# Two image layers on one core: the filling of the first pipeline rearranged

## The chip, the core and the metric

The kernel runs on one core of a Trainium2 chip. The time is the device time of one execution in microseconds (us). Before the change it is 3877.8 us, the median of three runs (3875.0 to 3879.05). The core has a matrix engine (PE, with weight loads shown apart as PEld), a vector engine (DVE), a scalar engine for activations (ACT), a general engine (POOL) and a queue engine (SP) that issues most transfers. Transfers move on 16 DMA engines shared by all queues. SP's transfers are plain copies. POOL issues those that add what they bring to what lies at the destination (accumulating transfers).

## What is computed

Input `x` has two images of 768 channels on 64 x 64 points. Two layers follow each other, each with a residual:

```python
x = x + mamba(_gn(x))      # layer 0
x = x + attention(_gn(x))  # layer 1
```

`_gn` is a group norm over 32 groups of 24 channels, with statistics over an image. Layer 0, cut to what matters:

```python
x = hs @ in_proj_w.T                          # 768 -> 1536 channels
xs = depthwise_conv3x3(x) + conv_b            # 9 taps per channel
xs = xs * sigmoid(xs)
dt, Bs, Cs = split(xs @ x_proj_w.T)           # 48 + 4 + 4
delta = softplus(dt @ dt_w.T + dt_b)
states = scan(exp(delta * A), delta * u * Bs) # along the 4096 points, 4 states
y = sum(states * Cs) + D * u
y = layernorm(y) * ln_g + ln_b                # over 1536 channels
out = y @ out_proj_w.T                        # 1536 -> 768
```

Layer 1 multiplies the normalized image by `W_qkv`, weighs it with a softmax over 12 heads, and multiplies it by `W_out`. The change does not touch it.

## The kernel before

An image is cut into 8 tiles of 8 rows (512 points); the two images make 16 tiles. The 1536 channels are 12 chunks of 128. A quantity number `g` counts tile times 12 plus chunk, 192 in all. One call of `step(g)` (line 894) does one piece of every stage of the pipeline for different numbers: the input product and row carry for number `n = g + 17`, the convolution taps for `a = g + 15`, the scan for `g`, and the output product for `g - 12`. The order is written out by hand (`tc.manual_schedule()`); each engine works through its own instructions in that order and waits where one needs another's result. The text counts the first steps as step 0 (`g = -17`) to step 15 (`g = -2`). In these, the filling, there is no scan and no output product.

Ahead of the filling (lines 876 to 892): 48 pieces of image 1 are loaded (`gn_load`, line 141) and DVE takes their statistics (`gn_piece`, L153). `gn_finish` (line 223) aggregates them per chunk (L225) and returns five parts of `gn_parts` (line 157). These average over the groups by matrix products with two constant matrices (`gavg_in`, loaded on L168; `gsel_in`, L174). In the four parts each matrix is loaded twice, by SP, into buffers taken from a pool of 46 (`slots`, with `take` and `give`). ACT then normalizes the six chunks of tile 0 (`norm_x`, L297) and computes the exponentials of `A_log` (L891, L892).

A step of the filling does, in this order:

- SP loads the input weights of the next number (`load_wi`, L303) into one of four buffers.
- PE multiplies image row 0 (`row0`, L325) and then the tile (`in_proj`, L336). Row 0 itself is loaded and normalized on ACT in step 0 (L318, L320).
- SP loads three pieces of image 2 (L148). DVE takes their statistics one step later, behind the taps.
- The taps of number `a`: ACT writes the middle tap into a PSUM bank (`tap_act`, L374). PE adds one tap by a product with a diagonal matrix that ACT made (`diag`, L369; `taps_pe`, L401). DVE adds the other seven (`taps_dve`, L415), the last into a buffer `u`. There is one such bank, so the taps of the next number wait for these.
- ACT evicts the input product with its carried rows (`in_proj_evict`, L348 to L351).
- Every fourth step ACT applies SiLU to four numbers between two table loads (`silu`, L420), and PE multiplies them by the projection weights (`x_proj_pair`, L427).

From number 15 on (`AHEAD`) the taps are divided in another way: ACT multiplies two or three taps into buffers `tm` (`taps_act`, L386). POOL adds them to each other by accumulating transfers (`taps_dma_sum`, L392) and adds the sum to `u` (`taps_dma`, L395). `DMA_TAPS`, `PE_TAPS` and `FILL_TAPS` name the taps.

The output weights are prepared in the filling too. Four loads (L242) bring all of them. In step 7 PE multiplies them by `ln_g` and `ln_b` (L250), 24 products of two rows by 384 columns. ACT copies the two rows (L254); PE then makes the output bias (L258) and the mean row spread over all partitions (L262). POOL scales each of the 12 chunks and subtracts the mean (L266, L267). SP stores them, two a step (L270), to a buffer in memory from which `load_wo` reads later.

When the filling ends, its buffers (`wg` among them) are given up and those of the scan take their place (`bc`, `ysum`, `tm`, `da`, `s`, lines 1056 to 1064). In the step of `g = -1` SP loads the rows of B and C spread over all partitions (`load_bc`, L447). In the step of `g = 0` DVE computes the first state product (L489), the first scan (L491), and so on.

Of the kernel before, what the change touches and what calls it, by code (L numbers as in the profile page):

```python
# [14 lines left out]
P = 128  # L15
# [4 lines left out]
NS = 4  # L20
# [28 lines left out]
PE_TAPS = ((), (1,), (), (1,))  # L49
FILL_TAPS = (1,)  # L50

# [15 lines left out]
def both_layers(  # L67
# [15 lines left out]
    nc.sync.dma_start(xsum, xsum_in)  # L83
    pick = wp.tile([2, P + 1], F32, name="pick")
    nc.sync.dma_start(pick, pick_in)
    xp_w = r0.tile([P, KI, XD2], F32, name="xp_w")
# [51 lines left out]

    pieces = {}

    def gn_load(b, v):
        k, h = divmod(v, L // 512)
        if b == 0:
            pieces[b, v] = take()
        else:
            tag, bufs = (("delta", 3), ("sq", 3), ("du", 2))[v % 8 // 3]
            pieces[b, v] = wk.tile([P, 512], F32, tag=tag, name=f"xg{b}_{v}", bufs=bufs)
        nc.sync.dma_start(pieces[b, v], xv[b][:, k, h * 512 : (h + 1) * 512])  # L148

    def gn_piece(b, v):  # L150
        k, h = divmod(v, L // 512)
        piece = pieces.pop((b, v))
        nc.vector.bn_stats(st_in[b][:, k, h, :], piece)  # L153
        if b == 0:
            give(piece)

    def gn_parts(name, mv, mean, rstd, then):


        st = {"held": []}  # L160

        def load(what):
            if what in st:
                return
            if what == "avg":
                st["held"] = [take()]
                st["avg"] = st["held"][0][:, : KM * G].rearrange("p (k g) -> p k g", g=G)
                nc.sync.dma_start(st["avg"], gavg_in)  # L168
            else:
                st["held"] = [take(), take()]  # L170
                st["sel"] = []
                for h, t in enumerate(st["held"]):
                    t = t[:G, : KM // 2 * P].rearrange("g (k p) -> g k p", p=P)
                    nc.sync.dma_start(t, gsel_in[:, h * (KM // 2) : (h + 1) * (KM // 2), :])  # L174
                    st["sel"] += [t[:, k, :] for k in range(KM // 2)]

        def done(what):
            st.pop(what)
            for t in st["held"]:
                give(t)  # L180

# [28 lines left out]
        def end():  # L210
            nc.vector.reciprocal(rstd, d)
            then()

        nothing = lambda: None
# [7 lines left out]

    def gn_finish(b):
        for k in range(KM):
            nc.vector.bn_aggr(mv_in[b][:, k, :], st_in[b][:, k, :, :])  # L225
        mean = gp.tile([P, KM], F32, name=f"xmean{b}")

        def then():
            nc.vector.tensor_mul(xbias[b], mean, xscale[b])
            nc.vector.tensor_scalar_mul(xbias[b], xbias[b], -1.0)  # L230
            nc.vector.tensor_scalar_mul(stats1[b][:, :, 2 * NT], mv_in[b][:, :, 0], -1.0)

        return gn_parts(f"x{b}", mv_in[b], mean, xscale[b], then)

    HM = DM // 2

    def out_weights_load(sp):
        wg = sp.tile([P, KI, DM], F32, name="wg")  # L240
        for k in range(0, KI, 3):
            nc.sync.dma_start(wg[:, k : k + 3, :], out_wT[k * P : (k + 3) * P, :].rearrange("(k p) m -> p k m", p=P))  # L242
        return wg

    def out_weights(sp, wg):

        gb = psO.tile([P, 2, 512], F32, tag="po", name="pgb")
        for e in range(2):
            for k in range(KI):
                nc.tensor.matmul(  # L250
                    gb[:2, e, :HM], pc[:, k, PC_G : PC_B + 1], wg[:, k, e * HM : (e + 1) * HM], start=(k == 0), stop=(k == KI - 1)
                )
        rows = sp.tile([2, 2, HM], F32, name="gb_rows")
        nc.scalar.copy(rows, gb[:2, :, :HM])  # L254
        rv = rows.rearrange("r e m -> r (e m)")
        pb = psS.tile([P, 512], F32, tag="st", name="pbo")
        for m in range(KM):
            nc.tensor.matmul(pb[:, m : m + 1], rv[:, m * P : (m + 1) * P], pick[:, P : P + 1], start=True, stop=True)  # L258
        nc.scalar.copy(bias_o, pb[:, :KM])
        wm = psO.tile([P, 2, 512], F32, tag="po", name="pwm")  # L260
        for e in range(2):
            nc.tensor.matmul(wm[:, e, :HM], pick[:, :P], rows[:, e, :], start=True, stop=True)  # L262
        wmean = sp.tile([P, 2, HM], F32, name="wmean")
        nc.scalar.copy(wmean, wm[:, :, :HM])
        for k in range(KI):
            nc.gpsimd.tensor_scalar_mul(wg[:, k, :], wg[:, k, :], pc[:, k, PC_G : PC_G + 1])  # L266
            nc.gpsimd.tensor_sub(wg[:, k, :], wg[:, k, :], wmean.rearrange("p e m -> p (e m)"))  # L267

# [42 lines left out]


    def row0(n):

        if n == 0:
            x0s["tile"] = take()
            x0s[0] = x0s["tile"][:, : KM * W].rearrange("p (k w) -> p k w", w=W)
            nc.sync.dma_start(x0s[0], xv[0][:, :, :W])  # L318
            for k in range(KM):
                nc.scalar.activation(  # L320
                    x0s[0][:, k, :], x0s[0][:, k, :], AF.Identity, bias=xbias[0][:, k : k + 1], scale=xscale[0][:, k : k + 1]
                )
        p0 = psZ.tile([P, 512], F32, tag="pz", name=f"pa0_{n}")
        for k in range(KM):
            nc.tensor.matmul(p0[:, :W], wis[n][:, k, :], x0s[0][:, k, :], start=(k == 0), stop=(k == KM - 1))  # L325
        nc.scalar.copy(carry[n][:, 1, :], p0[:, :W])
        if n == KI - 1:
            give(x0s.pop("tile"))
# [30 lines left out]
    def dma_taps(a):  # L359
        return DMA_TAPS[a % 4] if a >= AHEAD else ()  # L360

    def pe_taps(a):
        return PE_TAPS[a % 4] if a >= AHEAD else FILL_TAPS

# [16 lines left out]
    def taps_act(a):  # L381
        xs, c = xs_bufs[a % 2], a % KI
        tms[a] = (tm_bufs[a % 2], tm_bufs[2], tm_bufs[3 + a % 2])
        for tm, j in zip(tms[a], dma_taps(a)):
# [6 lines left out]
    def taps_dma_sum(a, q):  # L391
        nc.gpsimd.dma_start(tms[a][0], tms[a][q], accum_op=ALU.add)  # L392

    def taps_dma(a):
        nc.gpsimd.dma_start(us[a], tms.pop(a)[0], accum_op=ALU.add)  # L395

# [476 lines left out]
    norms = {}  # L873
    N_PIECE = KM * (L // 512)
    PER_STEP = 3
    with tc.manual_schedule():
        for v in range(N_PIECE):
            gn_load(0, v)
            gn_piece(0, v)
        for k in range(KM):  # L880
            load_x(0, k)
        load_wi(0)
        nc.sync.dma_start(xp_w, xp_wP)
        nc.sync.dma_start(dt_w, dt_wP)
        for load, pe, dve in gn_finish(0):
            load()
            pe()
            dve()
        for k in range(KM):
            norm_x(0, k)  # L890
        nc.scalar.activation(neg_a, pc[:, :, PC_A : PC_A + NS], AF.Exp)  # L891
        nc.scalar.mul(neg_a, neg_a, -1.0)  # L892

        def step(g, prep=None):
# [4 lines left out]
            if n + 1 < NQ0:  # L899
                load_wi(n + 1)  # L900
            elif NQ0 <= n + 1 < NQ0 + N_TAIL:
# [3 lines left out]
            if n < KI:  # L905
                row0(n)
            for q in range(v * PER_STEP, min((v + 1) * PER_STEP, N_PIECE)):
                gn_load(1, q)
# [19 lines left out]
            if BEHIND < g <= NQ0 + BEHIND and (g - BEHIND) % 4 == 0:  # L928
                out_evict(g)
            for q in range((v - 1) * PER_STEP, min(v * PER_STEP, N_PIECE)):  # L930
                if q >= 0:
                    gn_piece(1, q)
            if BEHIND + 2 < g and (g - BEHIND) % 4 == 2:
# [33 lines left out]
            elif n < NQ0 + N_TAIL:  # L967
# [4 lines left out]
                for k in {3: [0], 4: [1], 5: [2, 3, 4, 5]}.get(d[2], []):  # L972
                    norm_x1(0, d[1] + 1, k)
            if AHEAD <= a + 1 < NQ0:
                taps_act(a + 1)
# [9 lines left out]
            if do_b:  # L985
                du(g)
            late_tap = AHEAD <= a < NQ0 and len(dma_taps(a)) > 2
            if late_tap:
# [3 lines left out]
            if 0 <= g - 2 < NQ0:  # L992
                y_dma(g - 2, 1)
            if AHEAD <= a < NQ0 and not late_tap:
                taps_dma(a)
            if AHEAD <= a + 1 < NQ0:
                taps_dma_sum(a + 1, 1)
# [37 lines left out]
            if do_silu:  # L1035
                for q in range(0, 4, 2):
                    x_proj_pair(a - 4 + q)
            if (v - 1) * PER_STEP == N_PIECE:
                norms[g + 2] = gn_finish(1)
# [7 lines left out]
        with tc.tile_pool(name="l0st", bufs=1, side="right") as sp:  # L1047
            wg = out_weights_load(sp)
            for g in range(-AHEAD - 2, -1):
                step(g, (lambda: out_weights(sp, wg)) if g == -AHEAD + 5 else None)  # L1050
                if g >= -AHEAD + 7:
                    for k in ((g + AHEAD - 7) * 2, (g + AHEAD - 7) * 2 + 1):
                        if k < KI:
                            out_weights_store(wg, k)

# [173 lines left out]
```

## Time and profile before

| what | us |
|---|---|
| median of the three runs | 3877.8 |
| lowest and highest | 3875.0, 3879.05 |
| the profiled execution | 3880.97 |
| its span | 3879.2 |
| PE busy | 3643.6 |
| DVE busy | 2792.9 |
| ACT busy | 2459.8 |
| POOL busy | 1657.2 |
| first matrix product of row 0 starts | 63.87 |
| first state product starts | 227.60 |

All places in the profile are us from the start of the span. A row such as `L336 PE` belongs to line 336 of the kernel. The chain of waits is followed back from the last instruction, at each point to what released it; its pieces show start, length and what. A product in 32 bit is two records of PE. The granted clock is the share of PE's full clock in a stretch.

### The profile page before, as it was taken

To read this page: it belongs to the slowest core of one execution; us is meant where nothing else is said; L and a number is where in the kernel's file an instruction comes from. 1 tells how busy PE (TensorE), PEld (TensorE's weight loads), DVE (VectorE), ACT (ScalarE), POOL (GpSimd) and SP (SyncE) were. 2 spreads that over 40 slices of the span, in tenths; PEclk is the share of its full clock that TensorE was granted. 3 is DMA by queue.
4 is the path that set the end of the run, shared out by engine and by line. 5 is a ranking of instruction groups with operands and counts; after the bars stand their busy time and mean duration, and the time that the engine had idled before them with its cause. 6 is when DMAs were issued, how large, how long until landed. Compare 5 with 4: busy or idle time off the path is not lost.

```text
span 3879.2 us, 32882 instructions
## 1 busy us (share of the span) xinstructions
PE 3643.6 (94%) x9798; PEld 1512.8 (39%) x9798; DVE 2792.9 (72%) x2339; ACT 2459.8 (63%) x4667; POOL 1657.2 (43%) x1494
## 2 busy tenths in 40 slices
PE   4977999999999999999999999999999999998999
PEld 2422333333333333333433333333344444444444
DVE  5699999999999999999999999987400520005311
ACT  1378888888898888888888888886423511123000
POOL 0435556555655655655555655554300011111222
PEclk9988999999999999999999999999999999999999
DMA  7466898888888889889888898886543245442454
GB/s 278 160 177 134 187 205 180 201 202 194 203 182 200 205 188 207 179 202 213 172 203 183 202 206 184 198 176 168 146 126 129 68 145 154 150 140 83 142 179 154
DMA packets 321574, 679.65 MB, mean 175 GB/s; under 512 B 37378, under 2 KB 45572, under 8 KB 317300
## 3 DMA queue, kind: packets, MB, share of 16 engines
q0 software_dynamic: 139248, 253.56, 38.2%
q1 hardware_dynamic: 182148, 424.00, 33.4%
q8 instruction: 78, 1.28, 0.1%
q14 instruction: 100, 0.82, 0.1%
HBM read 393.77 MB, written 55.31 MB: 116 GB/s over the span
## 4 chain that ended last, share of the span: by engine, by line
DVE 45%; PE 34%; ACT 7%; issue 6%; DMA 5%; POOL 3%; SPq 0%; DVEq 0%; POOLq 0%; ACTq 0%
DVE s L491 17%; PE mm L665 13%; DVE acc L415 9%; PE mm L638 9%; DVE da L498 8%; DVE s L489 7%; PE pa L336 3%; PE po L551 3%; DMA tm<-tm 2%; PE pq L638 2%; DMA u<-tm 2%; POOL ysum L478 1%; DMA u<-ysum 1%; DVE u L563 1%; ACT da L466 1%
## 5 line engine op out<-in xcount | busy, mean ns | idle before, releaser
L551 PE MATMUL po<-u,w 128*128 128x512 f32 x2304 | 1047.8, 605 | 69.1 <-DVE u L563 68.7
L336 PE MATMUL pa<-u,w 128*128 128x512 f32 (+1 forms) x2304 | 1040.0, 601 | 0.0
L491 DVE TENSOR_TENSOR_SCAN s<-da,s 128x2052 f32<-128x2052 f32 x192 | 851.1, 4433 | 19.2 <-DVE s L489 0.5
L551 PEld LDWEIGHTS po<-u,w 128*128 128x128 f32 x2304 | 431.5, 192 | 673.8 <-issue 569.1
L336 PEld LDWEIGHTS pa<-u,w 128*128 128x128 f32 x2304 | 430.4, 192 | 591.4 <-issue 529.0
L478 POOL TENSOR_TENSOR ysum<-da 128x1024 f32<-128x1024 f32 x192 | 396.7, 2066 | 533.1 <-DVE da L498 506.9
L415 DVE SCALAR_TENSOR_TENSOR acc<-xs,pc,acc 128x512 f32<-128x512 f32 x753 | 567.8, 754 | 70.3 <-PE acc L401 50.3
L466 ACT ACTIVATE da<-dl,neg_a 128x512 f32<-128x512 f32 x768 | 489.6, 713 | 0.0
L660 POOL TENSOR_TENSOR w<-w,at 128x768 f32<-128x768 f32 x96 | 141.0, 1470 | 814.9 <-DMA w<-woutP 562.5
L392 POOL DMA_DIRECT2D tm<-tm x310 | 273.9, 885 | 500.5 <-ACT tm L386 444.9
L489 DVE TENSOR_TENSOR s<-du,bc 128x2048 f32<-128x2048 f32 x192 | 438.8, 2285 | 66.0 <-POOL du L470 63.8
L498 DVE TENSOR_TENSOR da<-s,bc 128x2048 f32<-128x2048 f32 x192 | 440.0, 2292 | 6.3
L485 POOL DMA_DIRECT2D u<-ysum x384 | 391.7, 1314 | 0.5 <-POOL ysum L478 0.3
L665 PE MATMUL mm<-u,w 128*128 128x512 f32 x684 | 320.8, 596 | 0.0
L386 ACT ACTIVATE tm<-xs,pc 128x512 f32<-128x512 f32 x487 | 317.7, 718 | 2.8 <-DMA tm<-tm 2.8
L674 DVE TENSOR_TENSOR u<-mm,u 128x512 f32<-128x512 f32 x59 | 40.8, 692 | 337.8 <-PE mm L665 337.8
L374 ACT ACTIVATE acc<-xs,pc 128x512 f32<-128x512 f32 x192 | 132.6, 690 | 211.7 <-DVE u L415 210.8
L470 POOL TENSOR_TENSOR du<-dl,u 128x512 f32<-128x512 f32 x192 | 258.7, 1348 | 0.0
L395 POOL DMA_DIRECT2D u<-tm x177 | 218.7, 1235 | 83.5 <-DMA tm<-tm 64.5
L665 PE MATMUL mm<-v,w 128*128 128x512 f32 x468 | 225.7, 593 | 0.0
L638 PE MATMUL mm<-u,w 128*128 128x512 f32 x456 | 214.4, 594 | 0.0
L665 PEld LDWEIGHTS mm<-u,w 128*128 128x128 f32 x684 | 129.3, 191 | 167.6 <-issue 167.4
(206 smaller groups left out, 4060.1 us busy)
## 6 DMA issues: line engine op xcount, KB each, us to landing
u<-ysum POOLq DMA_DIRECT2D x384, 256.0 KB, 5.8
tm<-tm POOLq DMA_DIRECT2D x310, 256.0 KB, 4.7
w<-in_wP SPq DMA_DIRECT2D x192, 384.0 KB, 4.3
w<-wo_dr SPq DMA_DIRECT2D x192, 384.0 KB, 5.1
u<-x SPq DMA_DIRECT2D x254, 256.0 KB, 4.3
u<-tm POOLq DMA_DIRECT2D x177, 256.0 KB, 5.8
w<-qkvP SPq DMA_DIRECT2D x96, 384.0 KB, 3.1
w<-woutP SPq DMA_DIRECT2D x96, 384.0 KB, 3.7
```

What stands on the lines that cost most here:

```text
L336: nc.tensor.matmul(pa[:, :nn], w[:, k, :], xts[i, k][:, :nn], start=(k == 0), stop=(k == KM - 1))
L386: nc.scalar.activation(tm.rearrange("p (h w) -> p h w", w=W), xs[:, dy : dy + TR, dx : dx + W], AF.Copy, scale=pc[:, c, PC_W + j : PC_W + ...
L415: nc.vector.scalar_tensor_tensor(dst, xs[:, dy : dy + TR, dx : dx + W], pc[:, c, PC_W + j : PC_W + j + 1], acc, ALU.mult, ALU.add)
L466: nc.scalar.activation(das[g % 2][:, n, 1:], deltas[g], AF.Exp, scale=neg_a[:, c, n : n + 1])
L478: nc.gpsimd.tensor_add(ysum[:, 0 : 2 + g % 2 : 1 + g % 2, :], da[:, 0:2, 1:], da[:, 2:4, 1:])
L485: nc.gpsimd.dma_start(us[g], ysums(g, n), accum_op=ALU.add)
L489: nc.vector.tensor_mul(s[:, :, 1:], dus.pop(g).unsqueeze(1).to_broadcast([P, NS, TL]), bc[:, :NS, :])
L491: nc.vector.tensor_tensor_scan(sf, das[g % 2].rearrange("p n l -> p (n l)"), sf, 0.0, ALU.mult, ALU.add)
L498: nc.vector.tensor_mul(das[g % 2][:, :, 1:], s[:, :, 1:], bc[:, NS:, :])
L551: nc.tensor.matmul(po[:, e, :], w[:, kk, e * P : (e + 1) * P], us[i * KI + k], start=(k == 0), stop=(k == KI - 1))
L638: nc.tensor.matmul(pa, w[:, k, :], x1s[b, j, k], start=(k == 0), stop=(k == KM - 1))
L665: nc.tensor.matmul(po, w[:, k, :], w1s[b, k, j], start=(k == 0), stop=(k == KM - 1))
```

## The change

- **Constants.** `gn_parts` gets `keep`: for image 1 each of the two constant matrices is loaded once and kept until the end. They are loaded directly behind the 48 pieces, ahead of tile 0, the weights and the rest.
- **Order ahead of the filling.** The load of row 0 and of input weights 1 and 2 go ahead of the filling; row 0 is normalized on DVE (`norm_x0`). The exponentials of `A_log` come after step 0.
- **Statistics of image 2.** Half of the 48 pieces are loaded ahead of the filling into the pool's buffers, and their statistics taken ahead of the taps. The other 24 go one or two a step.
- **Taps of the filling.** PE's tap 1 goes; taps 0 and 2 go to ACT and accumulating transfers, in buffers from the pool. DVE has six taps instead of seven.
- **Input weights** are loaded up to two steps ahead in the filling.
- **Output weights.** The four loads go to steps 2 to 5. The two rows are computed in three column groups of 256 (partitions 0, 32 and 64 of the result), in step 7; bias and mean follow in step 8, with a `pick` of 128 rows. ACT scales the chunks, POOL subtracts. One or two chunks a step, from step 8 to 15; their stores come a step later.

```diff
-FILL_TAPS = (1,)
+FILL_TAPS = (0, 2)
...
     def gn_load(b, v):
         k, h = divmod(v, L // 512)
-        if b == 0:
+        if v < N_EARLY[b]:
             pieces[b, v] = take()
...
+    def out_weights_load(wg, k):
+        nc.sync.dma_start(wg[:, k : k + 3, :], out_wT[k * P : (k + 3) * P, :].rearrange("(k p) m -> p k m", p=P))
+    MG = 2 * P
+    def out_weights_rows(wg, rows):
         gb = psO.tile([P, 2, 512], F32, tag="po", name="pgb")
-        for e in range(2):
-            for k in range(KI):
+        for k in range(KI):
+            for j in range(KM // 2):
                 nc.tensor.matmul(
-                    gb[:2, e, :HM], pc[:, k, PC_G : PC_B + 1], wg[:, k, e * HM : (e + 1) * HM], start=(k == 0), stop=(k == KI - 1)
+                    gb[32 * j : 32 * j + 2, 0, :MG], pc[:, k, PC_G : PC_B + 1], wg[:, k, j * MG : (j + 1) * MG],
+                    start=(k == 0), stop=(k == KI - 1),
                 )
+        for j in range(KM // 2):
+            nc.scalar.copy(rows[32 * j : 32 * j + 2, :], gb[32 * j : 32 * j + 2, 0, :MG])
+    def out_weights_mean(rows, wmean, pick):
         pb = psS.tile([P, 512], F32, tag="st", name="pbo")
+        wm = psO.tile([P, 2, 512], F32, tag="po", name="pwm")
+        for j in range(KM // 2):
+            for e in range(2):
+                m = 2 * j + e
+                nc.tensor.matmul(pb[:, m : m + 1], rows[:, e * P : (e + 1) * P], pick[:, j, P : P + 1], start=True, stop=True)
+            nc.tensor.matmul(wm[:, j // 2, j % 2 * MG : (j % 2 + 1) * MG], pick[:, j, :P], rows, start=True, stop=True)
+        nc.scalar.copy(wmean[:, : 2 * MG], wm[:, 0, :])
+        nc.scalar.copy(wmean[:, 2 * MG :], wm[:, 1, :MG])
         nc.scalar.copy(bias_o, pb[:, :KM])
...
-        for k in range(KI):
-            nc.gpsimd.tensor_scalar_mul(wg[:, k, :], wg[:, k, :], pc[:, k, PC_G : PC_G + 1])
-            nc.gpsimd.tensor_sub(wg[:, k, :], wg[:, k, :], wmean.rearrange("p e m -> p (e m)"))
+    def out_weights_scale(wg, wmean, k):
+        nc.scalar.activation(wg[:, k, :], wg[:, k, :], AF.Copy, scale=pc[:, k, PC_G : PC_G + 1])
+        nc.gpsimd.tensor_sub(wg[:, k, :], wg[:, k, :], wmean)
...
+    def norm_x0():
+        for k in range(KM):
+            nc.vector.tensor_scalar(
+                x0s[0][:, k, :], x0s[0][:, k, :], xscale[0][:, k : k + 1], xbias[0][:, k : k + 1], ALU.mult, ALU.add
+            )
...
     def dma_taps(a):
-        return DMA_TAPS[a % 4] if a >= AHEAD else ()
+        return DMA_TAPS[a % 4] if a >= AHEAD else FILL_TAPS
     def pe_taps(a):
-        return PE_TAPS[a % 4] if a >= AHEAD else FILL_TAPS
+        return PE_TAPS[a % 4] if a >= AHEAD else ()
...
-        tms[a] = (tm_bufs[a % 2], tm_bufs[2], tm_bufs[3 + a % 2])
+        tms[a] = (tm_bufs[a % 2], tm_bufs[2], tm_bufs[3 + a % 2]) if a >= AHEAD else (take(), take())
...
+    at = [0, 2, 3, 5, 6, 8, 9, 11, 12, 14, 15, 17, 18, 20, 21, 23, 24]
+    by_step = [range(N_PIECE // 2 + p, N_PIECE // 2 + q) for p, q in zip(at, at[1:])]
     with tc.manual_schedule():
         for v in range(N_PIECE):
             gn_load(0, v)
             gn_piece(0, v)
+        gn_aggregate(0)
+        parts = gn_finish(0)
+        for load, pe, dve in parts[:2]:
+            load()
         for k in range(KM):
             load_x(0, k)
         load_wi(0)
+        load_x0()
+        for n in (1, 2):
+            load_wi(n)
+        for v in range(N_EARLY[1]):
+            gn_load(1, v)
         nc.sync.dma_start(xp_w, xp_wP)
         nc.sync.dma_start(dt_w, dt_wP)
-        for load, pe, dve in gn_finish(0):
-            load()
+        for load, pe, dve in parts:
             pe()
             dve()
+        norm_x0()
         for k in range(KM):
             norm_x(0, k)
-        nc.scalar.activation(neg_a, pc[:, :, PC_A : PC_A + NS], AF.Exp)
-        nc.scalar.mul(neg_a, neg_a, -1.0)
+        for v in range(N_EARLY[1]):
+            gn_piece(1, v)
...
-            if AHEAD <= a < NQ0 and not late_tap:
+            if 0 <= a < NQ0 and not late_tap:
                 taps_dma(a)
-            if AHEAD <= a + 1 < NQ0:
+            if 0 <= a + 1 < NQ0:
                 taps_dma_sum(a + 1, 1)
...
+            first = -AHEAD - 2
+            ready_w = {8: (0,), 9: (1, 2), 10: (3,), 11: (4, 5), 12: (6, 7), 13: (8, 9), 14: (10,), 15: (11,)}
+            prep = {7: lambda: out_weights_rows(wg, rows), 8: lambda: out_weights_mean(rows, wmean, pick)}
+            for v in range(AHEAD + 1):
+                if 2 <= v < 6:
+                    out_weights_load(wg, 3 * (v - 2))
+                step(first + v, prep.get(v))
+                if v == 0:
+                    nc.scalar.activation(neg_a, pc[:, :, PC_A : PC_A + NS], AF.Exp)
+                    nc.scalar.mul(neg_a, neg_a, -1.0)
+                for k in ready_w.get(v, ()):
+                    out_weights_scale(wg, wmean, k)
+                for k in ready_w.get(v - 1, ()):
+                    out_weights_store(wg, k)
+            for k in ready_w[AHEAD]:
+                out_weights_store(wg, k)
```

## The prediction

> **What bounds the kernel now.** I read the page first (busy shares and forty slices), then busy time by stage, then the chain of waits in order of time through the first 260 us.
>
> ```profile
> PE 3643.6 (94%) x9798; PEld 1512.8 (39%) x9798; DVE 2792.9 (72%) x2339; ACT 2459.8 (63%) x4667; POOL 1657.2 (43%) x1494
> PE   4977999999999999999999999999999999998999
> ```
>
> PE carries the kernel; only the first slices leave it idle. The change touches only them. Busy time by stage:
>
> ```profile
> 39.70:63.90 24.20, 7.00 (x49) 6.72 (x49) 4.12 (x20) 6.73 (x12) 0.00 (x0) 1.00 1.02 365
> 128.10:158.30 30.20, 29.32 (x92) 11.80 (x91) 7.07 (x10) 3.81 (x9) 10.62 (x6) 0.89 0.24 75
> 227.60:380.00 152.40, 103.90 (x283) 39.89 (x282) 146.24 (x105) 125.95 (x228) 82.35 (x76) 0.81 0.66 133
> 380.00:2500.00 2120.00, 2038.85 (x5365) 810.45 (x5363) 2054.72 (x1354) 1823.36 (x3428) 1241.06 (x1151) 0.99 0.88 196
> ```
>
> (Columns: stretch, length, PE, PEld, DVE, ACT, POOL busy, clock, DMA share, GB/s.) From the first state product (DVE L489 at 227.6) on, DVE is 96 to 97% busy, so nothing there absorbs an earlier start: every us that 227.6 moves should reach the end. So I price that moment, called S. The chain to it:
>
> ```profile
> 40.39 7.33 DMA u<-gavg_in
> 57.33 4.33 ACT u L297 x6
> 61.66 1.28 ACT L891
> 63.39 0.43 ACT u L320
> 102.18 1.01 PE acc L401 x2
> 128.98 15.59 PE pgb L250 x48
> 144.59 0.80 ACT gb_rows L254
> 146.92 1.82 PE pwm L262 x4
> 148.74 2.75 PE pa L325 x12
> 151.50 6.81 PE pa L336 x12
> ```
>
> The group norm waits 7.3 us for its constants behind 2.7 MB of loads. ACT then serves six norms, a table load and image row 0 before PE starts at 63.87. Each step costs 7.5 us (row 0 1.28, product 5.21, tap 1.01). The output weights interrupt PE for 128.98 to 148.74. The page's rows of DMA queues and issues price the operation that the change adds to the filling (queue, packets, MB, share; then KB each and median us to landing):
>
> ```profile
> q0 software_dynamic: 139248, 253.56, 38.2%
> ...
> tm<-tm POOLq DMA_DIRECT2D x310, 256.0 KB, 4.7
> ...
> u<-tm POOLq DMA_DIRECT2D x177, 256.0 KB, 5.8
> ```
>
> **The change part by part.** I laid the changed order out engine by engine, each in its own order, with these durations.
>
> *Constants first.* SP issues them right behind image 1's pieces, so they land with the last piece, near 40. The averages then wait only for the six aggregates (end 41.2): 47.83 becomes 41.0, gain 6.8. The 9.5 us of averages to bias stay. The small load dropped at the start is worth 0 to 0.4; I take 0.
>
> *Row 0 on DVE, exponentials after step 0.* Six 128x64 operations on DVE cost about 1 us (the 128x6 ones cost 0.17 each), while ACT runs the six norms. Row 0 (2.8 at half pace, as now) starts near 51.3 and the first product after the sixth norm, 50.5 + 4.33 = 54.8, against 66.69. Cumulative gain 11.9. The table load and exponentials (1.8) move under step 1's product. Weights 1 and 2 and row 0 go ahead of 24 pieces; all land before use.
>
> *Half of image 2's statistics ahead.* 24 pieces x 256 KB at 404 GB/s (the rate of 20 to 40 us) are 15.6 us of queue, 24 x 0.635 = 15.2 us of DVE, from 51.3 to 66.5. Two more pieces queue behind them and two weight loads, so the first taps start near 68; step 2 needs them only then. Free, and each step keeps 1.5 pieces instead of 3 (0.9 us of DVE less).
>
> *Taps 0 and 2 by ACT and accumulating DMA, none on PE.* A step loses PE's 1.01, one of seven DVE taps (0.79) and ACT's diagonal (0.40). It gains two ACT products (1.94/3 = 0.65 each) and two POOL issues (L392 0.885, L395 1.235), with the accumulate's landing between them on POOL. PE then needs 1.28 + 5.21 = 6.5 a step, DVE 6 x 0.79 + 0.72 for ACT's product = 5.5, ACT 3.4. So PE bounds, and step 6's product, which ends at 117.2 now, ends at 100.2: cumulative gain 17.
>
> *The accumulate chain* is the new wait. POOL issues add a, then sum a+1, and add a+1 waits until sum a+1 has landed. The adds gate the SiLU of steps 6, 10 and 14, and behind SiLU stand ACT's product, its eviction and PE's x projection. An accumulate of 256 KB takes 38.2% x 3879 / 967 (253.56 MB in pieces of 256 KB) = 1.53 us of all DMA engines. Landing runs from 3.3 (best) over 4.7 (median) to 11.8 us. From the best landing 3.3 - 0.885 - 1.53 = 0.9 is latency, from the median 2.3; I take 1.4. One round is then issue 1.2 + 2 x 1.53 + 1.4 = 5.7 us alone, under 6.5. But in steps 2 to 5 SP now loads 1152 KB of output weights a step: with 384 KB of weights and 1.5 pieces that is about 5 us of DMA a step, plus 3.1 of accumulates, in 6.5 us. Sharing doubles the transfers: 1.2 + 6.1 + 1.4 = 8.7 a round. With the first sum issued at 70 and landed at 75, the fourth add is issued at 75 + 3 x 8.7 = 101 and lands at 107; ACT was ready for it at 99. PE's x projection waits from 100.2 to 107.7. So from step 6's product to step 7's: 7.5 + 1.87 + 1.28 + 5.2 + 2.9 for a slow clock after the wait = 18.8, against 10.9 now (117.2 to 128.1): loss 7.9, cumulative 9.1. Ends: a gain of 2.6 (5.7 a round, no wait) and a loss of 17 (11 a round). I take 7.9, as the load queue is full there. After step 6 POOL's subtractions stand between sums and adds; with 1.8 each they fit into the landing.
>
> The Trainium skill ("DMA: Bandwidth & Descriptors", section on queues, rings and completion order) says that each DMA engine round-robins between queues packet by packet. That speaks against this change, since loads would not yield to accumulates; no row of this trace has both queues isolated. By that rule the loss of 7.9 stands; if accumulates went first, the gain of 2.6 would.
>
> *Output weights' rows.* 72 records at 256 columns, 0.32 x 256/384 = 0.215 each, are 15.5 us one after another, or 5.2 with three column groups side by side. Row: L427, two groups of 64 columns, 8 records in 1.94 us instead of 8 x 0.43 = 3.4 (5.21 / 12 = 0.43 is a record of 512 columns). I take 5.2; the other end is 15.5. The means follow a step later (2.7 us on PE, counted there), so ACT's copies no longer stop PE, and the slow clock behind them (2.75 + 6.81 instead of 1.28 + 5.21) goes. From step 7's product to step 8's: 128.1 to 158.3 = 30.2 now, 5.2 + 1.28 + 5.2 = 11.7 after: gain 18.5 (8.2 by the other end), cumulative 27.6.
>
> *Scaling moved from POOL to ACT.* POOL loses 12 x 2.20. ACT gains 12 copies of 128x768 between 0.80 (L264) and 1.1 (0.78 for 512 columns, scaled up); I take 0.95. ACT's load over steps 8 to 15 becomes 8 x 3.4 + 2 x 5.1 (SiLU and tables) + 11.4 + 4.7 (norms) + 1.2 = 55 us, more than PE's 45. In order, with the waits on evictions, the means' 2.7 and one slow-clock stretch behind step 11's three norms (2.9), step 8's product to step 15's takes 59.6 (158.3 to 214.7 = 56.4 now): loss 3.2, ends a gain of 4 and a loss of 8.
>
> The same slow clock is in the Trainium skill ("TensorE: Matmul & The Clock Gate", Part 1): half rate after an idle window of about 3.4 us. Here row 0's 12 records took 2.82 us after idling and 1.45 in a run of work. By the rule an idle of 2 us would cost nothing and one of 7 about 2 to 3.
>
> *Stores a step late; the state products' inputs.* The last store (weights 11) now follows step 15's product on ACT, subtraction 1.8 and store 3.4 (page: 4.2 to landing). SP has the loads of B and C behind it, and their buffer lies where the weights lay. POOL's clearing of the decay buffers waits there too. From step 15's product, near 190: sum and copies to 193, the last copy at 195, subtraction 197, store 200, loads (median 6.5) 206. That is 15.6 against 214.7 to 227.6 = 12.9: loss 2.7, ends 0 and 8. SP's weight loads stand behind stores that wait for POOL; they are issued two steps ahead, which covers it.
>
> **Sum.** 17.0 - 7.9 + 18.5 - 3.2 - 2.7 = 21.7, so S at 206. The profiled execution is 3880.97 (span 3879.2), 3.2 above the median 3877.8. 3880.97 - 21.7 = 3859.3, so 3856 for a median.
>
> **The rivals.**
> 1. *The accumulates are never late* (5.7 to 6.5 a round). Speaks for it: median landing 4.7 with DMA 88% busy. Against: the load queue is full in steps 2 to 5. S near 198: 3880.97 - 29 - 3.2 = 3848.
> 2. *Half the gain:* groups run one after another (+10.3), or rounds of 9.5 to 10. S near 217: 3867. Against the first: L427.
> 3. *Slower: the accumulate chain sets the fill.* With rounds of P throughout, the last sum is issued at 70 + 14 P and S follows 16 us later (subtraction, store, loads): S = 86 + 14 P. It decides from P = 10.1; at 11 S is 240, 3890. For it: landings up to 11.8. Against: after step 6 loads fall to some 2.5 us a step.
> 4. *The gain is taken back* between 227.6 and 380 (clock 0.81, PE 68% busy), where PE's lead over DVE is rebuilt: no change, 3877. Against: DVE 96% busy there.
>
> **How the numbers follow.** Forecast (3851 to 3862) 0.48, rival 1 0.27, rival 2 0.13, rival 3 0.07, rival 4 0.05. Slower 0.07, same 0.05, faster 0.88; 0.2% (7.8 us) is about what a measurement can tell. Range 3842 to 3872: from S at 192 (no wait anywhere, ACT at 0.80 a copy) to S at 222 (groups one after another), which leaves some 0.17 out.
>
> **What would show it.** Averages at 41, first product near 55, steps of 6.5 up to step 6, a wait of ACT's L420 for the add's DMA at step 6, rows of some 5 us, S near 206, and 3650 us from S to the end as now. I am wrong if SiLU waits in every group, if the rows take 15 us, or if that last stretch grows.

## The result and the profile after

Median 3870.1 us (8 runs, 3864.9 to 3875.8) against 3879.4 (8 runs): ratio 0.9977, 95% interval 0.9967 to 0.9986, that is 5 to 13 us faster. The profiled execution has a span of 3866.9 us, 12.3 less than before. Forecast was a gain of 21.7 and a median near 3856: the direction holds, the size is too large, and 3870.1 lies above the 3851 to 3862 that were given the largest chance.

The page's busy shares and slices, then the queue and issue rows of the changed kernel:

```profile
PE 3631.4 (94%) x9794; PEld 1511.2 (39%) x9794; DVE 2783.4 (72%) x2331; ACT 2480.1 (64%) x4691; POOL 1655.0 (43%) x1512
...
PE   5867999999999999999999999999999999998999
...
q0 software_dynamic: 143568, 261.42, 40.2%
...
tm<-tm POOLq DMA_DIRECT2D x310, 256.0 KB, 4.7
u<-tm POOLq DMA_DIRECT2D x177, 256.0 KB, 5.9
```

PE gets to work within the first slice (5 instead of 4). Queue 0 carries 7.9 MB more: the 30 added accumulates of 256 KB. Busy time by stage (columns as in the prediction: stretch, length, PE, PEld, DVE, ACT, POOL, clock, DMA share, GB/s), from the averages to product 0, to product 6, 7, 8 and 15, to the first state product (S), to the second, and the run:

```profile
40.72:60.83 20.11, 17.16 (x74) 12.81 (x75) 12.74 (x37) 4.94 (x9) 0.00 (x0) 1.00 1.04 373
60.83:103.40 42.57, 40.86 (x147) 22.12 (x147) 33.94 (x50) 19.91 (x44) 6.21 (x7) 0.96 1.06 349
103.40:122.66 19.26, 13.18 (x35) 5.93 (x38) 8.80 (x13) 6.63 (x12) 4.32 (x5) 0.73 0.62 138
122.66:134.63 11.97, 11.97 (x99) 6.10 (x99) 6.11 (x9) 4.09 (x10) 1.72 (x2) 1.00 0.43 100
134.63:196.38 61.75, 53.49 (x156) 24.73 (x155) 36.89 (x52) 44.80 (x77) 32.03 (x25) 0.92 0.81 213
196.38:211.53 15.15, 13.09 (x33) 5.07 (x31) 5.18 (x8) 14.19 (x26) 5.87 (x7) 1.00 0.64 196
211.53:229.81 18.28, 6.91 (x18) 2.50 (x16) 14.07 (x15) 10.45 (x20) 5.92 (x6) 0.76 0.92 250
```

```profile
380.00:2500.00 2120.00, 2040.67 (x5373) 811.36 (x5372) 2053.49 (x1355) 1826.78 (x3433) 1240.27 (x1152) 0.99 0.89 196
```

Product 6 ends at 103.4 (before 117.2), product 7 at 122.7 (128.1), product 8 at 134.6 (158.3), product 15 at 196.4 (214.7), and S is at 211.5 (227.6): 16.1 gained at S where 21.7 was forecast. Then the first scan step takes 18.3 us instead of 14.8, so that the second state product has a gain of only 12.6. From there to the end both kernels take the same time within 0.3 us. The chain of waits (start, length, what) shows three places where accumulates or sums are waited for:

```profile
97.47 1.21 DMA u<-u
98.67 8.45 issue
107.14 3.62 DMA u<-u
110.78 0.73 ACT u L437
...
113.53 2.75 PE pa L337 x12
116.28 6.38 PE pa L348 x12
122.66 5.29 PE pgb L255 x72
...
177.97 6.75 DMA u<-u
...
213.50 4.65 issue
218.15 6.96 DMA tm<-tm
...
225.67 3.31 DMA u<-tm
```

The first (97 to 111) is the one of the prediction, before the SiLU of step 6. The row called "issue" is POOL standing before an add until the sum that it issued at 97.47 has landed, 9.1 us later. The second (178 to 185) is the same wait at step 14. The third (213 to 229) lies behind S; these are the sums and the add of the taps from number 15 on, which the kernel before has too. The rows (L255) cost 5.29 us.

### The profile page after: what moved, and what is told of

Read it like the earlier page. It is cut to its first block, busy times and chain, and to the rows that moved or that the text cites. A ratio compares the mean times of both kernels' runs of the same rounds, so it can differ in the third digit from the quotient of the medians.

```text
span 3866.9 us, 32976 instructions
## 1 busy us (share of the span) xinstructions
PE 3631.4 (94%) x9794; PEld 1511.2 (39%) x9794; DVE 2783.4 (72%) x2331; ACT 2480.1 (64%) x4691; POOL 1655.0 (43%) x1512
## 3 DMA queue, kind: packets, MB, share of 16 engines
q1 hardware_dynamic: 182048, 424.00, 33.5%
## 4 chain that ended last, share of the span: by engine, by line
DVE 40%; PE 32%; ACT 8%; issue 6%; DMA 6%; POOL 4%; SPq 0%; DVEq 0%; POOLq 0%; ACTq 0%
DVE s L508 16%; PE mm L682 13%; PE mm L655 9%; DVE acc L432 8%; DVE da L515 8%; DVE s L506 6%; PE po L568 3%; DMA tm<-tm 2%; PE pa L348 2%; DMA u<-tm 2%; PE pq L655 2%; DMA u<-ysum 2%; POOL ysum L495 1%; ACT da L483 1%; POOL du L487 1%
## 5 line engine op out<-in xcount | busy, mean ns | idle before, releaser
L432 DVE SCALAR_TENSOR_TENSOR acc<-xs,pc,acc 128x512 f32<-128x512 f32 x738 | 556.4, 754 | 73.1 <-ACT acc L386 44.7
L398 ACT ACTIVATE tm<-xs,pc 128x512 f32<-128x512 f32 x487 | 317.8, 718 | 5.5 <-DMA tm<-tm 4.2
L655 PE MATMUL mm<-u,w 128*128 128x512 f32 x456 | 214.4, 594 | 0.0
```

Source lines behind the costliest of these rows:

```text
L398: nc.scalar.activation(tm.rearrange("p (h w) -> p h w", w=W), xs[:, dy : dy + TR, dx : dx + W], AF.Copy, scale=pc[:, c, PC_W + j : PC_W + ...
L432: nc.vector.scalar_tensor_tensor(dst, xs[:, dy : dy + TR, dx : dx + W], pc[:, c, PC_W + j : PC_W + j + 1], acc, ALU.mult, ALU.add)
L655: nc.tensor.matmul(pa, w[:, k, :], x1s[b, j, k], start=(k == 0), stop=(k == KM - 1))
```

## The experiments

The theory under test: the accumulating transfers of the filling took the missing gain, because loads lengthen them, and they are waited for more often than the sum counted. Rivals: the output weights' stores at the end; the first taps, which are late behind image 2's early pieces; ACT's load of scaling. Each run is compared with the kernel before on the same chip. Input weights two steps ahead were never run alone.

**Stores sooner.**

```diff
-ready_w = {8: (0,), 9: (1, 2), 10: (3,), ... 14: (10,), 15: (11,)}
+ready_w = {8: (0, 1), 9: (2, 3), 10: (4, 5), 11: (6, 7), 12: (8, 9), 13: (10, 11)}
```

> The changed kernel with the output weights' chunks scaled and stored two a step in steps 8 to 13, instead of one or two in steps 8 to 15; all else as it is. In the changed kernel the last store leaves SP at 203.4, the loads of B and C follow at 205.9, and S is 211.53; the second state product comes 18.3 after it where a scan step later takes 12.9. If the stores at the end set S, and the loads of B and C that still run behind S set the long first scan step: loads of B and C right behind the projection's copy, near 200, S near 206, the second state product near 219 to 221 instead of 229.81, and the time 8 to 10 us below the changed kernel's, 3860 to 3862. If the end hangs on PE and ACT (the chain of adds, steps stretched by scaling): S within 2 us of 211.5, the time within 3 us of 3870. If ACT's denser scaling in steps 8 to 13 costs as much as it frees: product 15 ends some 4 us later than 196.4, the time near 3870.

Measured: 3869.5 us, ratio 0.9975 (0.9966 to 0.9984). SP issues B and C at 199.07 instead of 205.9, yet S comes at 213.77, 2.2 us later. The time is that of the second case, which expected S where it was. POOL's timeline (start, length, instruction, idle before):

```profile
199.94 0.86 POOL L404 DMA_DIRECT2D u<-u  x1 [4.64 <-ACT dg L381]
200.47 0.47 POOL L1107 MEMSET da<- 128x4 f32 x2
210.70 0.86 POOL L410 DMA_DIRECT2D u<-u  x1 [9.75 <-issue]
211.23 1.21 POOL L404 DMA_DIRECT2D tm<-tm  x1
211.79 1.94 POOL L487 TENSOR_TENSOR du<-dl,u 128x512 f32<-128x512 f32 x1
```

The last sum of the filling is issued at 199.94, right behind the 2 MB of B and C, and the add behind it stands until 210.70: the sum takes 10.2 us to land. `du`, which S needs, is queued behind that add. None of my cases had this cause: the stores were late, but taking them away only put the loads on top of the last sum. The first scan step is now 14.3, so the second state product gains 1.8.

**Tap 1 on PE again, no accumulates in the filling.**

```diff
-FILL_TAPS = (0, 2)   # in dma_taps, by ACT and accumulating transfers
+FILL_TAPS = (1,)     # in pe_taps; DVE has seven taps
```

> The changed kernel with the filling's taps as before: tap 1 on PE, seven on DVE, none by ACT and accumulating transfers; all else as changed. If the chain of adds is what took the missing gain (SiLU waits for its transfers at steps 6 and 14): steps of 7.5, step 6's product ends near 105 to 106 (103.4 in the changed kernel), but step 6 to 7 takes 11 to 13 instead of 19.2, so that product 7 ends near 118 (122.66) and product 15 near 190 (196.4); time 3 to 6 us below the changed kernel's. If the adds cost nothing in the end (what waits for them would wait for something else): every step is 1 us longer, S near 218, time 5 to 8 us above the changed kernel's, 3875 to 3878. If the end chain alone sets S: the time within 2 us.

Measured: 3864.6, ratio 0.9962 (0.9949 to 0.9974), 6 us better than the changed kernel against its own runs of before (15.3 below instead of 9.3). Product 6 to 7 takes 10.9 instead of 19.3, as the theory has it. But product 6 ends at 112.0, not 105 to 106, product 7 at 123.0 and product 15 at 198.4, not 118 and 190. So the time met the first case's 3 to 6 us and its path did not: at the second state product only 2.0 of the 6 us are there (227.8 against 229.81). PE's timeline:

```profile
68.77 5.37 PE L348 MATMUL pa<-u,w 128*128 128x512 f32 x12
77.71 2.05 PE L418 MATMUL acc<-xs,dg 128*128 128x512 f32 x2 [3.56 <-issue]
79.55 2.66 PE L337 MATMUL pa<-u,w 128*128 128x64 f32 x12
82.00 7.68 PE L348 MATMUL pa<-u,w 128*128 128x512 f32 x12
```

PE's own tap (L418) needs the PSUM bank that DVE's first taps hold to 76.8. Those start at 71.3 behind image 2's pieces. PE idles until 77.7 and then runs at half pace: step 3 takes 15.5 us.

**A quarter of the output weights' loads** (the other chunks are filled with ones).

```diff
-if 2 <= v < 6: out_weights_load(wg, 3 * (v - 2))
+if v == 2: out_weights_load(wg, 0)      # and ahead: nc.gpsimd.memset(wg[:, 3:, :], 1.0)
```

> The changed kernel with only the first of the four loads of output weights; the other nine chunks are filled with ones by POOL ahead of the filling, so the output weights' values are left out in three quarters. 3.5 MB less are loaded in steps 3 to 5, where the rounds of sum and add took 9 to 10 us. If the loads stretch the rounds (the prediction's account): rounds of 5.7 to 7 us, the fourth SiLU of step 6 waits less than 1 us for its transfer (5.02), step 6 to 7 takes 11 to 13 us instead of 19.2, product 7 ends near 115 (122.66). If the rounds are long of themselves (latency, POOL's order): rounds of 9 to 10 stay, and product 7 ends within 2 us of 122.7. The time follows product 7 only if the end chain lets it: 3863 if it does, 3870 if not.

Measured: 3862.6, ratio 0.9958 (0.9945 to 0.9970). POOL's adds of steps 2 to 5 in the changed kernel:

```profile
77.19 0.86 POOL L410 DMA_DIRECT2D u<-u  x1 [6.52 <-DMA xg<-x]
...
87.18 0.85 POOL L410 DMA_DIRECT2D u<-u  x1 [8.04 <-DMA wg<-out_wT]
...
96.93 0.86 POOL L410 DMA_DIRECT2D u<-u  x1 [8.01 <-DVE acc L432]
...
107.14 0.86 POOL L410 DMA_DIRECT2D u<-u  x1 [8.46 <-issue]
```

and with a quarter of the loads:

```profile
78.57 0.86 POOL L410 DMA_DIRECT2D u<-u  x1 [6.62 <-DVE acc L432]
...
85.81 0.85 POOL L410 DMA_DIRECT2D u<-u  x1 [5.49 <-DVE acc L432]
...
91.15 0.86 POOL L410 DMA_DIRECT2D u<-u  x1 [3.60 <-DVE acc L432]
...
99.67 0.86 POOL L410 DMA_DIRECT2D u<-u  x1 [6.77 <-DVE st_in L153]
```

Rounds of 10.0, 9.8 and 10.2 become 7.2, 5.3 and 8.5. The accumulates' median time to landing between 70 and 108 us falls from 7.1 to 5.0 us, product 6 to 7 from 19.3 to 10.0, and S comes at 199.6. So the loads do stretch the rounds. The fourth SiLU still waits 2.0 us (less than 1 was expected). The time fell by 8 where S fell by 12.

**16 early pieces instead of 24.**

```diff
-N_EARLY = (N_PIECE, N_PIECE // 2)
+N_EARLY = (N_PIECE, N_PIECE // 3)       # then two a step
```

> The changed kernel with 16 of image 2's pieces ahead of the filling instead of 24, and two a step afterwards instead of one or two. In the changed kernel DVE waits to 69.1 for pieces 24 and 25, which lie behind 24 pieces and the small weights in the queue, and the first taps start at 70.42; step 3's product comes late for it. If the late first taps cost the 3.2 us by which step 6's product (103.4) missed its forecast (100.2): first taps near 65, step 6's product near 100, the sums of steps 2 to 5 as late as now or 3 us sooner, time 0 to 3 us below the changed kernel's. If the chain of adds swallows it: step 6's product near 100, product 7 still near 122.7, time within 2 us. If the 8 pieces that move into steps 2 to 5 lengthen the rounds (2 MB more where the queue is full): product 7 near 125, time 2 to 4 us above.

Measured: 3868.9, ratio 0.9972 (0.9961 to 0.9983). DVE in the changed kernel, and with 16 pieces:

```profile
69.13 1.37 DVE L153 BATCH_NORM_STATS2 st_in<-xg 128x6 f32<-128x512 f32 x2 [2.31 <-DMA xg<-x]
70.42 3.90 DVE L432 SCALAR_TENSOR_TENSOR acc<-xs,pc,acc 128x512 f32<-128x512 f32 x5
```

```profile
64.78 1.36 DVE L153 BATCH_NORM_STATS2 st_in<-xg 128x6 f32<-128x512 f32 x2 [2.62 <-DMA xg<-x]
66.06 3.90 DVE L432 SCALAR_TENSOR_TENSOR acc<-xs,pc,acc 128x512 f32<-128x512 f32 x5
```

The first taps are 4.4 us earlier and product 6 ends at 100.4, where the prediction had 100.2. So 3.0 of the 3.2 us missing there are the late first taps. How they reach PE in the changed kernel (ACT's middle tap, then PE):

```profile
75.20 0.69 ACT L386 ACTIVATE acc<-xs,pc 128x512 f32<-128x512 f32 x1 [5.75 <-DVE u L432]
```

```profile
76.81 7.11 PE L348 MATMUL pa<-u,w 128*128 128x512 f32 x12 [1.71 <-ACT carry L363]
```

ACT's middle tap for the next number waits for the bank until 75.20, and the eviction that frees PE's next bank stands behind it. PE idles for 1.7 us, and the product behind that takes 7.11 instead of 5.37 (granted clock 0.81 from 75.1 to 83.9). Product 7 ends at 120.1, 2.5 us sooner; the adds take only a little of it back. The time is 11.0 below before instead of 9.3, which the intervals don't tell apart.

**The three together.** `FILL_TAPS`, `N_EARLY` and `ready_w` as in the three diffs above.

> The changed kernel with three things: the filling's tap 1 on PE and seven on DVE as before (no accumulating transfers in the filling), 16 of image 2's pieces early instead of 24, and the output weights' chunks scaled and stored two a step in steps 8 to 13. Each alone gave little: with the PE tap alone, step 3 took 15.6 us because PE's tap stood behind DVE's first taps at 71.3; with 16 pieces alone the adds at step 6 stayed (19.7 us from product 6 to 7); with sooner stores alone B and C were loaded at 199 but the last sum of taps landed 10 us late beside them, and du stood behind its add on POOL. If all three gains were lost to transfers that share the queue, they come together here: step 3 in 7.5 us, product 7 near 115, product 15 near 190, S near 201 to 203, the second state product near 217, time 3853 to 3856. If each only uncovers another wait of the same size: S near 208 to 211, time 3862 to 3865.

Measured: 3857.4, ratio 0.9942 (0.9930 to 0.9955). Step 3 takes 7.6, product 7 ends at 114.9, product 15 at 192.0, S is at 204.8 and the second state product at 219.1. This is a little short of the first case. The gains come together: 24.5 below the kernel before, where one by one they stood at 10.5, 15.3 and 11.0, the changed kernel's 9.3 included. Added to it one by one they would have made 18.2.

**The adds put back into that version.** One difference: `FILL_TAPS = (0, 2)` by ACT and accumulating transfers.

> The version with the PE tap, 16 early pieces and chunks two a step on ACT, with the one difference that taps 0 and 2 are again made by ACT and accumulating transfers and PE's tap is gone (the changed kernel with 16 early pieces and sooner stores). It prices the adds alone, against that version's product 7 at 114.9, product 15 at 192.0, S at 204.84, second state product at 219.11 and 24.5 us below the kernel before. If the adds are the price: steps of 6.5 bring product 6 to 100.4 (104.0), but product 6 to 7 takes 19 to 20 us, product 7 ends near 120, the last add lands 10 us late beside B and C, S near 208 to 211, second state product near 225 to 226; and, as in the four kernels with adds so far, POOL stalls once more at the 37th scan step and 3 to 6 us more are lost behind: time 10 to 13 us above that version, some 12 to 14 us below the kernel before. If the adds only looked dear beside 24 early pieces and late stores: S within 2 us of 204.84 and the time within 3 us of that version's.

Measured: 3866.7, ratio 0.9965 (0.9953 to 0.9978), 13.9 below before instead of 24.5. Stages of this kernel from product 6 to 7, from product 15 to S, and from S to the second state product:

```profile
99.40:120.80 21.40, 14.53 (x36) 6.43 (x38) 10.08 (x15) 6.64 (x12) 4.34 (x5) 0.68 0.63 140
195.90:214.03 18.13, 16.89 (x42) 6.49 (x41) 5.84 (x10) 14.91 (x28) 4.06 (x6) 1.00 0.83 258
214.03:228.29 14.26, 3.08 (x8) 1.05 (x6) 13.98 (x14) 9.63 (x16) 7.07 (x7) 0.72 0.71 147
```

and the same three stages without the adds:

```profile
104.00:114.90 10.90, 9.65 (x35) 4.64 (x36) 6.71 (x10) 3.47 (x9) 0.00 (x0) 1.00 0.32 108
192.00:204.84 12.84, 12.84 (x32) 5.03 (x31) 9.50 (x13) 11.05 (x20) 2.33 (x2) 1.00 0.74 271
204.84:219.11 14.27, 7.96 (x20) 2.88 (x18) 13.99 (x15) 10.95 (x22) 6.08 (x7) 0.91 0.79 193
```

The adds gain 4.6 us up to product 6 by shorter steps and 2.0 from product 7 to 15. They lose 10.5 from product 6 to 7, where the clock of the stretch is 0.68, and 5.3 from product 15 to S, where the last sum takes 10.7 us to land beside B and C. Net: 9.2 us at the second state product, 10.6 by the medians. S came later than I had expected (214.0, not 208 to 211). The further loss of 3 to 6 us behind it did not come: 14.1 gained at the second state product, 13.9 at the end.

**Scaling on POOL again**, in the version without adds.

```diff
-nc.scalar.activation(wg[:, k, :], wg[:, k, :], AF.Copy, scale=...)
+nc.gpsimd.tensor_scalar_mul(wg[:, k, :], wg[:, k, :], ...)
```

> As the version with the PE tap, 16 early pieces and chunks two a step, but POOL scales the chunks as it did before (2.2 us each, ahead of its subtraction of 1.8), so ACT loses 12 x 0.95 in steps 8 to 13. It prices the move of the scaling to ACT. If ACT's load is what stretches products 8 to 15 (61.75 us in the changed kernel, 62.6 with the PE tap, 56.4 before): product 15 comes 4 to 6 us sooner than in that version, and so does S; time 3848 to 3851. If ACT has room without the taps' products (3.0 us a step of its own, 1.9 for two chunks, in steps of 7.5): product 15 within 1.5 us of that version, the same time within 2 us; and if POOL is late with the last chunks (24 us more on POOL over six steps), later by 2 to 5 us.

Measured: 3853.6, ratio 0.9931 (0.9919 to 0.9944): 28.3 below the kernel before, the fastest of all. Product 15 comes at 187.3 and S at 200.15, both 4.7 sooner, as the first case had it; the time fell by 3.7, a little less than expected. Product 8 to 15 (stage columns as above):

```profile
128.40:187.30 58.90, 54.17 (x169) 25.35 (x169) 45.36 (x63) 29.75 (x59) 45.88 (x25) 1.00 0.58 188
```

ACT is busy for 29.75 us of 58.9. With the scaling on ACT the stretch from product 8 to 15 takes 64.3.

**Rows alone, on the kernel before.** Only `out_weights_rows` in three column groups and `out_weights_mean` a step later; POOL scales as before.

> The kernel before with only the two rows of the output weights in three column groups (step 7) and bias and mean a step later; scaling stays on POOL, loads and stores stay where they were. The prediction's term for this is 18.5 us from product 7 to product 8 (30.2 before). If it was sized right and nothing behind it waits: product 8 near 140, S near 209, time 18 us below the kernel before, near 3861. If POOL's scaling, which starts with the mean, sets the end (12 chunks of 4.0 us from about 146, to 194, and the stores behind it): product 8 near 140 but S near 212 to 216, time 3865 to 3869. If PE's gain is taken by SiLU or statistics behind it: S near 220.

Measured: 3867.8, ratio 0.9965 (0.9952 to 0.9979). Product 7 to 8 takes 12.8 instead of 30.2: 17.4 gained. The means then stretch step 9 to 10.0. Product 15 to S stays 12.9, so POOL's scaling does not set the end: S at 213.2 and the time met that case's numbers, its cause is another.

**Constants alone, on the kernel before.** `keep`, the loads ahead, `norm_x0` and the later exponentials.

> The kernel before with only the constants first, row 0 loaded ahead and normalized on DVE, and the exponentials after step 0. The prediction's term: 11.9 us at the first product. If it carries through: first product ends near 61.5 (73.2 before), product 6 near 105.3 (117.2), S near 215.7, time 12 us below the kernel before, near 3868. If the loads are what the earlier steps then wait for (the output weights' 4.6 MB are loaded ahead of the weights of steps 1 to 3 here): the first product early, but product 3 within 4 us of 94.7, time within 4 us of 3880.

Measured: 3872.0, ratio 0.9972 (0.9963 to 0.9981). The first product ends at 60.2 (13.0 sooner). Step 1 then waits for its weights behind the output weights' loads and runs at half pace, and product 6 ends at 107.5, 9.7 sooner. That is nearer the first case than the second, whose wait is there but costs 3.3 us and not all of the gain.

**Both on the kernel before.** The edits of the last two.

> The kernel before with two parts of the change together: constants first with row 0 on DVE and exponentials later, and the output weights' rows in column groups with the mean a step later. Taps, statistics, loads, scaling and stores stay as before. Alone they took 9.9 and 14.1 us off the median; at S they gave 9.7 and 14.4. If they add up: S near 203.5, second state product near 217.6, time 24 us below the kernel before, within 5 us of the best version so far (28.3 below), so that the other parts of the change are worth next to nothing or less. If one uncovers a wait for the other (loads of the output weights not there at step 7, POOL's 48 us of scaling setting the last stores): S near 207 to 212, time 16 to 20 us below.

Measured: 3859.6, ratio 0.9946 (0.9932 to 0.9959), 21.0 below, between the two cases. Two parts of the change give more than twice what all of it gives, and three quarters of the 28.3 of the fastest version.

All in one table (us; ends of products and start of the second state product from each trace; P15 to 2nd: from product 15's end to the second state product; below: median against the kernel before on the same chip):

| kernel | P6 | P7 | P15 | 2nd | P15 to 2nd | below |
|---|---|---|---|---|---|---|
| before | 117.2 | 128.1 | 214.7 | 242.4 | 27.6 | 0 |
| changed | 103.4 | 122.7 | 196.4 | 229.8 | 33.4 | 9.3 |
| stores sooner | 103.0 | 123.4 | 196.1 | 228.0 | 32.0 | 10.5 |
| PE tap | 112.0 | 123.0 | 198.4 | 227.8 | 29.4 | 15.3 |
| quarter of loads | 102.7 | 112.6 | 185.2 | 218.6 | 33.4 | 17.3 |
| 16 early | 100.4 | 120.1 | 193.9 | 227.4 | 33.5 | 11.0 |
| three together | 104.0 | 114.9 | 192.0 | 219.1 | 27.1 | 24.5 |
| adds put back | 99.4 | 120.8 | 195.9 | 228.3 | 32.4 | 13.9 |
| POOL scales | 104.6 | 115.6 | 187.3 | 214.4 | 27.1 | 28.3 |
| rows alone | 117.7 | 128.6 | 200.3 | 227.8 | 27.4 | 14.1 |
| constants alone | 107.5 | 118.4 | 205.1 | 232.2 | 27.1 | 9.9 |
| both | 110.6 | 121.6 | 193.3 | 220.6 | 27.2 | 21.0 |

The column P15 to 2nd sorts the kernels: 32.0 to 33.5 with adds in the filling, whether the stores are late or sooner; 29.4 without adds and with late stores; 27.1 to 27.6 with neither.

The gain at the second state product and the gain of the median agree within 1.2 us in the kernels without adds, and in the one with the adds put back. In the other four with adds the median keeps 3 to 6.5 us less (changed: 12.6 and 9.3; quarter of loads: 23.8 and 17.3). Some 2 us of that are found (last section); where the rest goes is open.

## Why the prediction was right or wrong

- *Constants first: right.* Averages at 40.7 (41 forecast), first product at 53.9 (54.8).
- *Half of image 2's statistics ahead, costed at nothing: wrong by 3.2 us.* The prediction had the two pieces behind the 24, but no wait for their transfer. DVE stood 2.3 us for it, so the first taps started at 70.4, not 68. Taps that start 1.7 us sooner, at 68.7, would not have held up PE (an estimate from PE's idle time before step 3's product), so "step 2 needs them only then" was right and the 68 was not. Step 3's product came late and ran slowly behind the idle time. The prediction reckoned that an idle of 2 us costs nothing; here 1.7 us of idling were followed by a product 1.7 us longer, while in the run with a quarter of the loads 1.4 us were followed by one of normal length (5.42). The run with 16 pieces gives 3.0 of the 3.2 back.
- *The accumulate chain: mechanism right, size wrong, and this is the main miss.* At step 6 the forecast of 18.8 us from product 6 to 7 was close (19.3), which is partly luck: rounds took 10 us and not 8.7, but product 6 was late too. With product 6 on time the runs show 19.8 (16 early) and 21.4 (adds put back). And I charged the chain once. It is waited for at step 14 again (6.75 us in the chain of waits): product 14 to 15 takes 18.4 with the adds put back and 12.4 without. Shorter steps before it make up for that (7.1 us from product 8 to 14). What nothing makes up for is the end: once the stores are sooner, the last sum stands beside B and C, and `du` behind its add (5.3 us). In the changed kernel itself B and C are issued after the last sum, which lands in 3.3 us, and S waits for B and C. In the prediction the taps' part nets to a loss of 2.8 (5.1 gained by steps, 7.9 lost); with and without adds the runs differ by 9.2 at the second state product and 10.6 in the median. That price is the one beside 16 early pieces and sooner stores.
- *The rule on queues* (the Trainium skill, "DMA: Bandwidth & Descriptors", on queues, rings and completion order: engines take packets from queues in turn) agrees in direction with this trace. With 3.5 MB less in the load queue the accumulates land in 5.0 instead of 7.1 us, so loads do not yield to them. That the turns go packet by packet no run here shows.
- *Rows in column groups: right.* 5.29 us against 5.2, product 7 to 8 in 11.97 against 11.7; alone 17.4 against 18.5.
- *Scaling on ACT: right in sign, too small.* Product 8 to 15 took 61.75 us, 5.4 more than before, where 3.2 more was forecast. Two versions without adds that differ in the scaling alone differ by 5.4 there too, and by 4.7 at S.
- *The end: right up to S, wrong behind it.* Product 15 to S took 15.15 (15.6 forecast). "Every us that S moves should reach the end" failed in the first scan step: 18.3 instead of 14.8. All four kernels with late stores have S 5.0 to 5.6 us behind the issue of B and C and a first scan step of 16.3 to 19.0; all others have 9.8 or more and 14.3 to 14.8. The loads at the end are then still running when POOL sums the next taps: in the changed kernel the first sum lands after 9.6 us and the next two after 7.0 and 7.9, in the kernel before after 8.2, 3.4 and 6.0.
- *Sum:* 21.7 - 3.2 (first taps) - 0.4 (step 6 to 7) - 0.3 (rows) - 2.2 (steps 9 to 15) + 0.5 (to S) - 3.5 (first scan step) = 12.6, the gain at the second state product. The profiled executions keep 12.3 of it, the medians show 9.3; the interval of the medians, 5 to 13, holds both.
- *The rivals.* The adds were late, so the first falls. (Its S near 198 only drops the loss of 7.9; with the prediction's own gain of 2.6 for no wait it would be near 195.) The second had rounds of 9.5 to 10, and those came (9.8 to 10.2), with S at 211.5 rather than 217; its 3867 is the nearest of the forecasts to the time, but by a loss behind S that it did not have. The third fails: from step 7 on POOL's sums wait for ACT's products (L398), not ACT for the sums, until step 14. The fourth is partly seen, but within one scan step, and beside loads that still run; that it comes from PE's lead no run shows.

## What to carry to other kernels

An accumulating transfer in a chain costs more than its own wait: list every place that waits for it, and everything that its engine's queue holds up behind it, and price each beside the loads that run there. Read a gain at the first point where the work repeats (here the second state product), not at the first instruction of the new stage. A change of several parts can hide good parts behind one bad one: putting the bad one back into the version with the three together priced it at 9 to 11 us, while undoing it alone in the changed kernel showed 6 (2.0 at the second state product), as other waits covered it there.

## What the runs showed of the hardware that was not expected

- A 256 KB accumulate issued right behind 2 MB of loads kept POOL standing for 9.8 and 10.2 us before the next add (two kernels; it landed after 10.2 and 10.7); the best landing of one takes 3.3.
- All five kernels with adds in the filling show POOL standing 7.3 to 7.8 us before the same sum in scan step 37, put down to "issue". The seven others show 5.3 to 5.8 there, waiting for ACT. POOL of the changed kernel, then of the kernel before:

```profile
719.19 0.85 POOL L404 DMA_DIRECT2D tm<-tm  x1 [7.83 <-issue]
```

```profile
727.09 0.86 POOL L392 DMA_DIRECT2D tm<-tm  x1 [5.31 <-ACT tm L386]
```

  It costs some 2 us there: ACT's product was ready at 716.9. Why is open, as nothing that the trace shows is waited for. In the kernel before a subtraction of 128 x 6 on DVE took 3.52 us at 1831 where the changed kernel's took 0.17, which goes the other way. Single executions hold such stalls of 2 to 4 us, as large as the parts that were priced here, so each part was read at its own place in the trace.
